# Attention values of two half-used row tiles, multiplied on two halves of the TensorE array

## The chip, the core and the metric

The kernel runs on one core of a Trainium2 chip. A core has five engines, each with its own instruction queue: TensorE (PE, matrix products; its weight loads are shown apart as PEld), VectorE (DVE), ScalarE (ACT), GpSimd (POOL) and SyncE (SP, which issues DMAs here). Matrix products write to PSUM, eight banks of 128 partitions × 512 fp32 values; DVE and ACT copy results from there to SBUF, the working memory. The metric is the device time in microseconds (us).

## The reference

A transformer block on x of shape (2, 512, 512), in fp32: attention, a layer norm of x plus its result, a gated feed-forward net of width 1376, and again a layer norm of the sum. The attention has 32 query heads of 128 values and 8 key/value heads, so four query heads share one key head:

```python
q = (x @ Wq.T).reshape(b, s, H, HD).transpose(0, 2, 1, 3)     # H = 32
k = (x @ Wk.T).reshape(b, s, HKV, HD).transpose(0, 2, 1, 3)   # HKV = 8
v = (x @ Wv.T).reshape(b, s, HKV, HD).transpose(0, 2, 1, 3)
q = _rmsnorm(q, q_norm_w)
k = _rmsnorm(k, k_norm_w)
scores = jnp.einsum('bkgqd,bksd->bkgqs', qg, k) / math.sqrt(HD)
bias = jnp.where(rel > 0, NEG_INF, slopes[:, :, None, None] * rel)
attn = jax.nn.softmax(scores + bias[None], axis=-1)
out = jnp.einsum('bkgqs,bksd->bkgqd', attn, v)
```

`rel` is key position minus query position: a query sees only keys up to its own place. What a product computes for later keys is nothing but zeros.

## The kernel before, in words

The sequence of 512 tokens is cut into four blocks of 128. A *unit* is (g, b, i): key head g (8), batch b (2), block i (4); there are 64 units. Two neighbouring units, i = 0 and 1 or i = 2 and 3, form a *pair* p, 32 in all; inside a pair r is 0 for the even block and 1 for the odd one.

For each pair, `project` computes queries, keys and values of both blocks, `heads` normalises and transposes them and copies the value rows into `v` (one 128 × 128 slab for each block, on ACT or POOL). `scores` and `attend` then run for each of the two units, and `project_out` multiplies the pair's attention result by the output weights and adds it to `y`. Projections use a seven-product scheme for 2 × 2 block matrices (`seven`, line 566), whose sums of operands (`so`, `to`, `tq`) and additions to results go through the helper at line 518 on DVE or POOL.

The 128 queries of a unit and their four heads make 512 rows of scores. They stand in four *row tiles* a = 0 to 3 of 128 rows: 32 neighbouring queries with all four heads. Row tile a of block i needs keys 0 to w = 128 i + 32 (a + 1), so on its own block of keys (the diagonal) tile 0 needs 32 keys, tile 1 needs 64, tile 2 needs 96 and tile 3 all 128. In `scores`, for each tile: a product into a bank `sc` (line 875), bias and maximum on DVE (line 884), exp and row sum on ACT (line 900); then a reciprocal `rden` of the four sums on DVE (line 915), and for each tile one multiplication by it on POOL (line 924), in place in `pr`. `pr` of block i has i + 1 slabs of 128 columns; what no tile writes was set to zero once at the start (line 479).

In `attend`, for each block of keys j up to i: four PE transposes, one for each tile, into a bank `pt` (line 943), and a copy of the whole bank to `prT` in SBUF (lines 641 on ACT or 643 on DVE). Then the products `pa` add up over j, each with 128 rows of values as weights and all 512 columns of `prT` moving (line 966); the result is copied, with a reordering of the columns, to `aT`, from which `project_out` reads. On the diagonal, too, all four tiles are transposed over 128 keys and multiplied with 128 rows of values.

PSUM: three banks `f` for projections, two `sc`, two `pt` (all transposes), one `po` (the attention results).

The order of the work is not that of the program text. Each piece is added to a list with the engines that may do it, an assumed cost, a priority, and the keys that it reads and writes; `emit` plays these through and hands out the piece that could start first, picks the engine, and takes buffers from rings as earlier holders are done. So a change in one piece can move others, on every engine, also in the feed-forward stage. DMAs go through SP's queue; the diff touches none.

Of the kernel before, what the change touches and what calls it, by code (L numbers as in the profile page):

```python
# [13 lines left out]
ALU = mybir.AluOpType  # L14
# [3 lines left out]
P = 128  # L18
B, S, DM = 2, 512, 512
H, HKV, HD = 32, 8, 128  # L20
G = H // HKV
# [9 lines left out]
NQ = P // Q  # L31
W3 = 3 * HD
WO = DM // 2
NTH = S // 2
RMS_EPS = 1e-6
LN_EPS = 1e-5
NEG_INF = -1e30
# [9 lines left out]
def pe(n):  # L47
    return max(0.14, n / 600)


TR = 0.107
# [14 lines left out]
def pool_ts(n):  # L66
    return 0.3 + 0.00095 * n
# [164 lines left out]
def post_ln_block(  # L232
# [18 lines left out]
    nc = tc.nc  # L251
# [4 lines left out]
    W = Work()  # L256
# [13 lines left out]
    def ring(stage, name, bufs, shape, dtype=F32, gate=None):  # L270
        r = Ring(name, bufs, shape, dtype, gate)
        rings.setdefault(stage, []).append(r)
        return r
# [6 lines left out]
    r_pt = ring("psum", "pt", 2, [P, S])  # L280
    r_po = ring("psum", "po", 1, [P, S])
# [33 lines left out]
    r_aT = ring("att", "aT", 2, [P, 2, G, P])  # L315
    r_so = ring("att", "so", 1, [P, 4, 2, P])
    r_rel = ring("att", "rel", 1, [P, S])
    r_pr = [ring("att", f"pr{i}", 1, [P, NQ, (i + 1) * P]) for i in range(NTB)]

    for stage, side in (("all", "left"), ("qkv", "left"), ("att", "right")):  # L320
# [8 lines left out]
    ident, nhalf, rel = fixed(r_id, "ident"), fixed(r_nh, "nhalf"), fixed(r_rel, "rel")  # L329
# [145 lines left out]
    for i in range(NTB):  # L475
        W.add(
            {"DVE": 0.1 + 0.00085 * NQ * (i + 1) * P},
            -8.0 + i,
            lambda e, i=i: nc.vector.memset(pr_of[i].tile, 0.0),
            (),  # L480
            [(pr_of[i], a) for a in range(NQ)],
        )

    bias = {}
# [148 lines left out]

    c_of, qTs, kTs, vs, prTs, aTs = {}, {}, {}, {}, {}, {}

    def copy_op(n, prio, dst, src, reads, writes, who=("ACT", "DVE")):
        def fn(e):
# [108 lines left out]
    def heads(p, prio):  # L748

        g, b, i = pairs[p]  # L750
        cb = c_of[p]
        c = lambda r: cb[:, r].rearrange("p n w -> p (n w)")
        if i == 0:
            kTs[g, b] = Buf(r_kT, f"kT_{g}_{b}")
            vs[g, b] = Buf(r_v, f"v_{g}_{b}")
        kT, v = kTs[g, b], vs[g, b]
        sq = Buf(r_sq, f"sq_{p}")
        ms, inv = Buf(r_ms, f"ms_{p}"), Buf(r_inv, f"inv_{p}")
        nh = 2 * (G + 1)
        for r in range(2):  # L760
            W.add(
                {"ACT": act(5 * HD) + 0.05},
                prio,
                lambda e, r=r: nc.scalar.activation(  # L764
                    sq[:, r].rearrange("p h d -> p (h d)"), c(r)[:, : 5 * HD], AF.Square
                ),
                [(cb, (r, 0)), (cb, (r, 1))],
                [(sq, r)],
            )
        W.add(  # L770
            {"DVE": 1.5},
            prio,
            lambda e: nc.vector.tensor_reduce(ms.tile, sq.tile, AX.X, ALU.add),
            [(sq, 0), (sq, 1)],
            [A(ms)],
        )
        W.add(
            {"DVE": 0.2},
            prio,
            lambda e: nc.vector.tensor_scalar(  # L780
                ms.tile, ms.tile, 1.0 / HD, RMS_EPS, ALU.mult, ALU.add
            ),
            [A(ms)],
            [A(ms)],
        )
        rsqrt(
            lambda: inv.tile.rearrange("p r h -> p (r h)"),
            lambda: ms.tile.rearrange("p r h -> p (r h)"),
            nh,
            prio,  # L790
            A(inv),
            A(ms),
        )
        for r in range(2):
            tensor(
                5 * HD,
                prio,
                lambda r=r: sq[:, r],
                lambda r=r: c(r)[:, : 5 * HD].rearrange("p (h d) -> p h d", h=G + 1),
                lambda r=r: inv[:, r].unsqueeze(2).to_broadcast([P, G + 1, HD]),  # L800
                ALU.mult,
                [(cb, (r, 0)), (cb, (r, 1)), A(inv)],
                [(sq, r)],
            )
            copy_op(
                HD,
                prio + 0.2,
                lambda r=r: v[:, i + r, :],
                lambda r=r: c(r)[:, 5 * HD :],
                [(cb, (r, 1))],  # L810
                [(v, i + r)],
                ("ACT", "POOL"),
            )
        for r in range(2):
            key = f"{g}_{b}_{i + r}"
            pt = Buf(r_pt, f"ptq_{key}")
            qT = Buf(r_qT, f"qT_{key}")
            qTs[g, b, i + r] = qT

            def transposes(e, r=r, pt=pt):  # L820
                for h, k in enumerate((0, 1, 3, 4)):
                    nc.tensor.transpose(pt[:, ts(h, P)], sq[:, r, k, :], ident.tile)  # L822

            W.add({"PE": 4 * TR}, prio + 0.4, transposes, [(sq, r), A(ident)], [A(pt)])

            def evict(e, pt=pt, qT=qT):
                src = pt.tile.rearrange("p (h a r) -> p a h r", h=G, a=NQ)
                if e == "ACT":
                    nc.scalar.activation(qT.tile, src, AF.Copy, scale=qw.tile)
                else:  # L830
                    nc.vector.tensor_scalar_mul(qT.tile, src, qw.tile)

            W.add(
                {"ACT": act(S, True), "DVE": dve(S) + 0.05},
                prio + 0.4,
                evict,
                [A(pt), A(qw)],
                [A(qT)],
            )
        ptk = Buf(r_pt, f"ptk_{p}")  # L840

        def transposes_k(e):
            for r in range(2):
                nc.tensor.transpose(ptk[:, ts(r, P)], sq[:, r, 2, :], ident.tile)

        W.add({"PE": 2 * TR}, prio + 0.4, transposes_k, [(sq, 0), (sq, 1), A(ident)], [A(ptk)])
        W.add(
            {"DVE": 0.48},
            prio + 0.4,
            lambda e: nc.vector.tensor_scalar_mul(  # L850
                kT[:, i * P : (i + 2) * P], ptk[:, : 2 * P], kw.tile
            ),
            [A(ptk), A(kw)],
            [(kT, i), (kT, i + 1)],
        )
# [3 lines left out]
    def scores(u, prio):  # L859
# [9 lines left out]
        for a in range(NQ):  # L869
# [46 lines left out]
            [(den, a) for a in range(NQ)],  # L916
            [A(rden)],
        )
        for a in range(NQ):
            w = i * P + (a + 1) * Q  # L920
            W.add(
                {"POOL": pool_ts(w)},
                prio,
                lambda e, a=a, w=w: nc.gpsimd.tensor_scalar(  # L924
                    pr[:, a, :w], pr[:, a, :w], rden[:, a : a + 1], 1.0, ALU.mult, ALU.mult
                ),
                [(pr, a), A(rden)],
                [(pr, a)],
            )

    def attend(u, prio):

        g, b, i = u
        key = f"{g}_{b}_{i}"
        pr, v = pr_of[i], vs[g, b]
        p, r = divmod(units.index(u), 2)
        for j in range(i + 1):
            pt, prT = Buf(r_pt, f"pt_{key}_{j}"), Buf(r_prT, f"prT_{key}_{j}")
            prTs[u, j] = prT

            def transposes(e, j=j, pt=pt):
                for a in range(NQ):
                    nc.tensor.transpose(pt[:, ts(a, P)], pr[:, a, ts(j, P)], ident.tile)  # L943

            W.add(
                {"PE": NQ * TR},
                prio,
                transposes,
                [(pr, a) for a in range(NQ)] + [A(ident)],
                [A(pt)],  # L950
            )
            copy_op(
                S,
                prio,
                lambda prT=prT: prT.tile,
                lambda pt=pt: pt.tile,
                [A(pt)],
                [A(prT)],
            )
        po = Buf(r_po, f"pa_{key}")  # L960
        for j in range(i + 1):
            prT = prTs[u, j]
            W.add(
                {"PE": pe(S)},
                prio + 0.4,
                lambda e, j=j, prT=prT: nc.tensor.matmul(  # L966
                    po.tile, lhsT=v[:, j, :], rhs=prT.tile, start=(j == 0), stop=(j == i)
                ),
                [A(prT), (v, j)] + ([A(po)] if j else []),
                [A(po)],  # L970
            )
        if r == 0:
            aTs[p] = Buf(r_aT, f"aT_{p}")
        aT = aTs[p]
        copy_op(
            S,
            prio + 0.4,
            lambda: aT[:, r].rearrange("p h (a r) -> p a h r", a=NQ),
            lambda: po.tile.rearrange("p (a h r) -> p a h r", a=NQ, h=G),
            [A(po)],  # L980
            [(aT, r)],
        )

# [24 lines left out]
    def project_out(p, prio):  # L1010
# [6 lines left out]
            lambda j: so[:, j],  # L1017
            lambda r, k: aT[:, r, 2 * k : 2 * k + 2, :],
            lambda j: (so, j),
            lambda r, k: [(aT, r)],  # L1020
        )

        def a_ap(f, ch):
            return aT[:, f[0], 2 * f[1] + ch, :] if isinstance(f, tuple) else so[:, f, ch, :]

        def a_keys(f):
            return [(aT, f[0])] if isinstance(f, tuple) else [(so, f)]

        def b_ap(f, ch):
            if isinstance(f, tuple):  # L1030
# [475 lines left out]
```

## Time and profile before

| What | Value |
|---|---|
| median of 3 runs | 1091.03 us (1090.96 to 1091.54) |
| the profiled execution's own time | 1091.2 us |
| its span | 1089.1 us |
| mean granted TensorE clock | 0.997 |
| transposes `pt` (line 943) | 640 |
| products `pa` (line 966), records | 320, all 128 × 512 |
| evictions `prT` | 107 on ACT, 587 ns each; 53 on DVE, 690 ns each |
| evictions `aT` | 38 on ACT, 586 ns each; 26 on DVE, 691 ns each |
| normalising on POOL (line 924) | 256, 627 ns each on average |

The span is the time from the first to the last instruction in the profile; the execution's own time is 2.1 us longer. A row of the groups reads: line, engine, operation, out<-in with shapes, count, then busy time and the mean length of one in ns, then how long the engine had been idle just before, and what ended that. Busy times of PE are modelled at their ends, so that the distance between two starts tells what an instruction costs there. In a table by stretches, the columns are the stretch, its length, and for PE, PEld, DVE, ACT and POOL the busy time and the number of instructions, then the granted clock, the DMA share and GB/s.

### The profile page before, as it was taken

How to read it: one execution, taken by the hardware profiler on the slowest of the kernel's cores; microseconds unless marked ns; L12 is line 12 of the kernel's file. 1: busy time of each engine (PE TensorE's matmuls, PEld its weight loads, DVE VectorE, ACT ScalarE, POOL GpSimd, SP SyncE). 2: the span in 40 equal slices, each digit the busy share in tenths (PEclk: the TensorE clock that was granted, in tenths of full speed). 3: DMA queues.
4: the chain of work that ended last, by engine and by line, in shares of the span. 5: the costliest groups of instructions: out<-in, count | busy, mean ns of one | idle time of the engine just before them, and what ended most of it. 6: DMA issues, size and time to landing. Idle time of an engine off the chain costs nothing.

```text
span 1089.1 us, 13052 instructions
## 1 busy us (share of the span) xinstructions
PE 1070.1 (98%) x4548; PEld 762.2 (70%) x4548; DVE 670.2 (62%) x1563; ACT 411.4 (38%) x1017; POOL 481.3 (44%) x600
## 2 busy tenths in 40 slices
PE   8999999999999999999999999999999999999997
PEld 5667676767676767676766666666666778887886
DVE  7756565656564656465656565657585666677554
ACT  2543334434434343444333434344444434433100
POOL 9444444344534453444344435454573443245130
PEclk9999999999999999999999999999999999999999
DMA  8210011001100120011001100100101013220011
GB/s 280 79 46 14 1 39 59 1 1 40 59 0 1 39 59 1 1 39 59 1 1 40 58 1 1 39 1 1 39 1 29 12 39 97 73 85 20 1 39 39
DMA packets 44144, 38.92 MB, mean 36 GB/s; under 512 B 3664, under 2 KB 36432, under 8 KB 44080
## 3 DMA queue, kind: packets, MB, share of 16 engines
q1 hardware_dynamic: 42352, 37.05, 11.0%
q10 hardware_dynamic: 1728, 1.05, 0.4%
q8 instruction: 36, 0.59, 0.2%
q14 instruction: 28, 0.23, 0.1%
HBM read 35.99 MB, written 2.10 MB: 35 GB/s over the span
## 4 chain that ended last, share of the span: by engine, by line
PE 86%; DVE 5%; POOL 5%; DMA 2%; ACT 1%; issue 1%; SPq 0%; POOLq 0%; DVEq 0%; ACTq 0%
PE pa_q L566 13%; PE pa L966 10%; PE sc L875 10%; PE pa_o L566 9%; PE pa_h L566 6%; PE pt L943 6%; PE pb_q L566 6%; PE pb_o L566 5%; PE pc_q L566 4%; PE pa_d L566 3%; PE pb_h L566 3%; PE ptq L822 2%; DVE tq L518 2%; PE pc_o L566 2%; POOL inv L504 2%; POOL pr L924 2%
## 5 line engine op out<-in xcount | busy, mean ns | idle before, releaser
L924 POOL TENSOR_SCALAR pr<-pr,rden 128x32 f32<-128x32 f32 (+15 forms) x256 | 155.8, 627 | 148.6 <-DVE rden L915 148.0
L900 ACT ACTIVATE pr<-pr,nmax 128x32 f32<-128x32 f32 (+15 forms) x256 | 131.9, 516 | 95.4 <-DVE nmax L884 95.2
L966 PE MATMUL pa<-prT,v 128*128 128x512 f32 x320 | 164.2, 595 | 0.0
L875 PE MATMUL sc<-kT,qT 128*128 128x160 f32 (+15 forms) x512 | 148.9, 402 | 0.0
L884 DVE CUSTOM_DVE_ANT_0 pr<-sc,bias 128x32 f32<-128x32 f32 (+15 forms) x256 | 108.9, 436 | 28.0 <-PE sc L875 25.3
L875 PEld LDWEIGHTS sc<-kT,qT 128*128 128x128 f32 x512 | 90.2, 190 | 47.8 <-issue 29.6
L641 ACT COPY c<-pa_q 128x384 f32<-128x384 f32 x101 | 48.3, 478 | 135.3 <-PE pa_q L566 130.4
L943 PEld LDWEIGHTS pt<-ident,pr 128*128 128x128 f32 x640 | 76.4, 141 | 26.7 <-issue 9.7
L943 PE MATMUL pt<-ident,pr 128*128 128x128 f32 x640 | 91.5, 275 | 0.9 <-POOL pr L924 0.3
L566 PE MATMUL pa_q<-tq,sx 128*128 128x384 f32 x248 | 90.4, 487 | 1.4 <-POOL pr L924 1.4
L641 ACT COPY prT<-pt 128x512 f32<-128x512 f32 x107 | 60.5, 587 | 79.1 <-PE pt L943 78.9
L504 POOL TENSOR_TENSOR inv<-ms,nhalf 128x10 f32<-128x10 f32 x32 | 62.9, 1965 | 53.4 <-DVE ms L780 53.2
L518 DVE TENSOR_TENSOR y<-y,pa_o 128x256 f32<-128x256 f32 x128 | 53.6, 419 | 50.7 <-PE pa_o L566 49.9
L643 DVE COPY prT<-pt 128x512 f32<-128x512 f32 x53 | 36.2, 690 | 61.8 <-PE pt L943 61.7
L764 ACT ACTIVATE sq<-c 128x640 f32<-128x640 f32 x64 | 47.2, 737 | 69.1 <-DVE c L518 67.3
L518 DVE TENSOR_TENSOR c<-pb_q,c 128x384 f32<-128x384 f32 x62 | 34.3, 554 | 61.9 <-PE pb_q L566 58.1
L966 PEld LDWEIGHTS pa<-prT,v 128*128 128x128 f32 x320 | 56.6, 190 | 22.0 <-issue 4.9
L643 POOL COPY v<-c 128x128 f32<-128x128 f32 x50 | 16.0, 321 | 124.1 <-DVE c L518 124.1
L566 PE MATMUL pa_o<-to,so 128*128 128x256 f32 x256 | 65.8, 380 | 0.3 <-POOL pr L924 0.3
L566 PEld LDWEIGHTS pa_q<-tq,sx 128*128 128x128 f32 x248 | 45.9, 192 | 27.5 <-POOL pr L924 2.6
L566 PEld LDWEIGHTS pa_o<-to,so 128*128 128x128 f32 x256 | 47.0, 190 | 20.2 <-issue 9.9
L641 ACT COPY gu<-pa_h 128x256 f32<-128x256 f32 (+1 forms) x88 | 32.1, 370 | 71.5 <-PE pa_h L566 54.8
(152 smaller groups left out, 2048.3 us busy)
## 6 DMA issues: line engine op xcount, KB each, us to landing
w<-in_wqt_dram SPq DMA_DIRECT2D x32, 256.0 KB, 4.2
wo<-in_wot_dram SPq DMA_DIRECT2D x8, 1024.0 KB, 5.5
wi<-in_gwt_dram SPq DMA_DIRECT2D x14, 256.0 KB, 2.8
wi<-in_uwt_dram SPq DMA_DIRECT2D x14, 256.0 KB, 3.2
wdi<-in_dwt_dram SPq DMA_DIRECT2D x10, 256.0 KB, 3.3
y<-in_x_dram SPq DMA_DIRECT2D x1, 2048.0 KB, 12.9
out_dram<-o SPq DMA_DIRECT2D x8, 256.0 KB, 2.0
w<-in_wkt_dram SPq DMA_DIRECT2D x7, 256.0 KB, 4.9
```

Source lines behind the costliest of these rows:

```text
L504: lambda e: nc.gpsimd.tensor_tensor(dst(), src(), nhalf[:, :n], ALU.pow),
L518: lambda e: vec[e].tensor_tensor(dst(), a(), b(), alu),
L566: nc.tensor.matmul(bank[:rows, :width], lhsT=a(fa, c), rhs=b(fb, c), start=(fresh and c == 0), stop=(c == depth - 1), skip_group_check=True,)
L641: nc.scalar.copy(dst(), src())
L643: vec[e].tensor_copy(dst(), src())
L764: lambda e, r=r: nc.scalar.activation(sq[:, r].rearrange("p h d -> p (h d)"), c(r)[:, : 5 * HD], AF.Square),
L875: lambda e, a=a, w=w, sc=sc: nc.tensor.matmul(sc[:, :w], lhsT=qT[:, a, :, :], rhs=kT[:, :w], start=True, stop=True),
L884: lambda e, a=a, w=w, sc=sc: nc.vector.tensor_tensor_reduce(out=pr[:, a, :w], in0=sc[:, :w], in1=bg[:, S - w :], scale=-1.0, scalar=MAX_IN ...
L900: lambda e, a=a, w=w: nc.scalar.activation(pr[:, a, :w], pr[:, a, :w], AF.Exp, bias=nmax[:, a : a + 1], scale=-1.0, accum_out=den[:, a : a ...
L924: lambda e, a=a, w=w: nc.gpsimd.tensor_scalar(pr[:, a, :w], pr[:, a, :w], rden[:, a : a + 1], 1.0, ALU.mult, ALU.mult),
L943: nc.tensor.transpose(pt[:, ts(a, P)], pr[:, a, ts(j, P)], ident.tile)
L966: lambda e, j=j, prT=prT: nc.tensor.matmul(po.tile, lhsT=v[:, j, :], rhs=prT.tile, start=(j == 0), stop=(j == i)),
```

## The change

Row tiles 0 and 1 need at most the first 64 keys of their own block. After the change these two tiles of the even block and of the odd block of a pair share one diagonal slab: that of the odd block, whose columns 64 to 127 are unused by its tiles 0 and 1. POOL's multiplication for tiles 0 and 1 of the even block writes the 64 diagonal columns there (into `pr` of the odd block) and, for i = 2, a second multiplication does the 256 earlier columns in place. The even block's diagonal then has two transposes in place of four; the odd block's four, in the order 2, 3, 0, 1, of which the last two carry both blocks: after transposing, rows 0 to 63 hold the odd block's keys and rows 64 to 127 the even block's.

The diagonal products `pa` take only tiles 2 and 3 (256 columns). Tiles 0 and 1 get two more products of 64 rows × 256 columns: rows 0 to 63 of the array with the odd block's values into a bank `px` (of the ring `pt`), and rows 64 to 127 with the even block's values into `pz` (of the ring `po`). For the second, the first 64 value rows of the even block are copied to partitions 64 to 127 (`v2`, on ACT or POOL). Both results are added to `aT` on DVE, but for the even block with i = 0, which has no earlier keys: there it is a copy.

```diff
+    r_vs = ring("att", "vs", 2, [P, HD])
...
+        v2 = Buf(r_vs, f"vs_{p}")
+        v2s[p] = v2
+        copy_op(
+            HD,
+            prio + 0.2,
+            lambda: v2[P // 2 :, :],
+            lambda: c(0)[: P // 2, 5 * HD :],
+            [(cb, (0, 1))],
+            [A(v2)],
+            ("ACT", "POOL"),
+        )
...
         for a in range(NQ):
             w = i * P + (a + 1) * Q
-            W.add(
-                {"POOL": pool_ts(w)},
-                prio,
-                lambda e, a=a, w=w: nc.gpsimd.tensor_scalar(
-                    pr[:, a, :w], pr[:, a, :w], rden[:, a : a + 1], 1.0, ALU.mult, ALU.mult
-                ),
-                [(pr, a), A(rden)],
-                [(pr, a)],
-            )
+            pieces = [(0, w, pr, 0, [(pr, a)])]
+            if i % 2 == 0 and a < 2:
+                pieces = [(i * P, H2, pr_of[i + 1], (i + 1) * P + H2, [(pr_of[i + 1], ("x", a))])]
+                if i > 0:
+                    pieces.append((0, i * P, pr, 0, [(pr, a)]))
+            for c0, n, to, c1, keys in pieces:
+                W.add(
+                    {"POOL": pool_ts(n)},
+                    prio,
+                    lambda e, a=a, c0=c0, n=n, to=to, c1=c1: nc.gpsimd.tensor_scalar(
+                        to[:, a, c1 : c1 + n],
+                        pr[:, a, c0 : c0 + n],
+                        rden[:, a : a + 1],
+                        1.0,
+                        ALU.mult,
+                        ALU.mult,
+                    ),
+                    [(pr, a), A(rden)],
+                    keys,
+                )
...
+            tiles = (2, 3) if j == i and r == 0 else (2, 3, 0, 1) if j == i else (0, 1, 2, 3)
...
+            def transposes(e, j=j, pt=pt, tiles=tiles):
+                for k, a in enumerate(tiles):
+                    nc.tensor.transpose(pt[:, ts(k, P)], pr[:, a, ts(j, P)], ident.tile)
...
+            n = S // 2 if j == i else S
             W.add(
-                {"PE": pe(S)},
+                {"PE": pe(n)},
                 prio + 0.4,
-                lambda e, j=j, prT=prT: nc.tensor.matmul(
-                    po.tile, lhsT=v[:, j, :], rhs=prT.tile, start=(j == 0), stop=(j == i)
+                lambda e, j=j, prT=prT, n=n: nc.tensor.matmul(
+                    po[:, S - n :],
+                    lhsT=v[:, j, :],
+                    rhs=prT[:, :n],
+                    start=(j == 0),
+                    stop=(j == i),
+                    skip_group_check=True,
                 ),
...
+        prT, v2 = prTs[u, i], v2s[p]
+        banks = (Buf(r_pt, f"px_{key}"), Buf(r_po, f"pz_{key}"))
+
+        def halves(e):
+            for k, (bank, val) in enumerate(zip(banks, (v[:, i, :], v2.tile))):
+                nc.tensor.matmul(
+                    bank[:, : S // 2],
+                    lhsT=val[k * H2 : (k + 1) * H2],
+                    rhs=prT[k * H2 : (k + 1) * H2, S // 2 :],
+                    start=True,
+                    stop=True,
+                    tile_position=(k * H2, 0),
+                )
+
+        W.add(
+            {"PE": 0.7},
+            prio + 0.4,
+            halves,
+            [A(prT), (v, i), A(v2)],
+            [A(bank) for bank in banks],
+        )
+        for k, bank in ((1, banks[0]), (0, banks[1])):
+            key_k = [(aT, (k, 0))]
+            if i - 1 + k == 0:
+                copy_op(
...
+            else:
+                tensor(
+                    S // 2,
+                    prio + 0.4,
+                    lambda k=k: cells(k, 0, 2),
+                    lambda k=k: cells(k, 0, 2),
+                    lambda bank=bank: rows(bank, 0, 2),
+                    ALU.add,
...
```

More of the change, by code (lines that the diff above doesn't have):

```diff
@@ L34 @@
 NTH = S // 2
+H2 = P // 2
 RMS_EPS = 1e-6
@@ L480, in post_ln_block @@
             (),
-            [(pr_of[i], a) for a in range(NQ)],
+            [(pr_of[i], a) for a in range(NQ)] + [(pr_of[i], ("x", a)) for a in range(2)],
         )
@@ L632, in sums_o @@
         )
-    c_of, qTs, kTs, vs, prTs, aTs = {}, {}, {}, {}, {}, {}
+    c_of, qTs, kTs, vs, v2s, prTs, aTs = {}, {}, {}, {}, {}, {}, {}
     def copy_op(n, prio, dst, src, reads, writes, who=("ACT", "DVE")):
@@ L939, in attend @@
             prTs[u, j] = prT
[L941 to L946, printed above, removed]
-                prio,
[L948 to L956, printed above, removed]
+            tiles = (2, 3) if j == i and r == 0 else (2, 3, 0, 1) if j == i else (0, 1, 2, 3)
+            reads = [(pr, a) for a in tiles]
+            if j == i and r:
+                reads += [(pr, ("x", a)) for a in range(2)]
+            def transposes(e, j=j, pt=pt, tiles=tiles):
+                for k, a in enumerate(tiles):
+                    nc.tensor.transpose(pt[:, ts(k, P)], pr[:, a, ts(j, P)], ident.tile)
+            n = len(tiles)
+            W.add({"PE": n * TR}, prio, transposes, reads + [A(ident)], [A(pt)])
+            copy_op(
+                n * P,
+                prio,
+                lambda prT=prT, n=n: prT[:, : n * P],
+                lambda pt=pt, n=n: pt[:, : n * P],
                 [A(pt)],
@@ L974, in attend @@
         aT = aTs[p]
+        a0 = 0 if i else 2
+        cells = lambda r, lo, hi: aT[:, r].rearrange("p h (a r) -> p a h r", a=NQ)[:, lo:hi]
+        rows = lambda t, lo, hi: t.tile.rearrange("p (a h r) -> p a h r", a=NQ, h=G)[:, lo:hi]
         copy_op(
-            S,
+            (NQ - a0) * P,
             prio + 0.4,
-            lambda: aT[:, r].rearrange("p h (a r) -> p a h r", a=NQ),
-            lambda: po.tile.rearrange("p (a h r) -> p a h r", a=NQ, h=G),
+            lambda: cells(r, a0, NQ),
+            lambda: rows(po, a0, NQ),
             [A(po)],
-            [(aT, r)],
+            [(aT, (r, h)) for h in range(a0 // 2, 2)],
         )
+        if r == 0:
+            return
+        prT, v2 = prTs[u, i], v2s[p]
[20 more added lines that the diff above has]
+            if i - 1 + k == 0:
+                copy_op(
+                    S // 2,
+                    prio + 0.4,
+                    lambda k=k: cells(k, 0, 2),
+                    lambda bank=bank: rows(bank, 0, 2),
+                    [A(bank)],
+                    key_k,
+                )
+            else:
+                tensor(
+                    S // 2,
+                    prio + 0.4,
+                    lambda k=k: cells(k, 0, 2),
+                    lambda k=k: cells(k, 0, 2),
+                    lambda bank=bank: rows(bank, 0, 2),
+                    ALU.add,
+                    [A(bank)] + key_k,
+                    key_k,
+                    ("DVE",),
+                )
     def accumulate(t, prio):
@@ L1019, in project_out @@
             lambda j: (so, j),
-            lambda r, k: [(aT, r)],
+            lambda r, k: [(aT, (r, 0)), (aT, (r, 1))],
         )
@@ L1026, in a_keys @@
         def a_keys(f):
-            return [(aT, f[0])] if isinstance(f, tuple) else [(so, f)]
+            return [(aT, (f[0], 0)), (aT, (f[0], 1))] if isinstance(f, tuple) else [(so, f)]
         def b_ap(f, ch):
```

## The prediction

> **What bounds the kernel now.** I read the totals first, then the chain that ended last, then the groups of the two steps concerned, then the timeline of TensorE for the real price of one instruction. The page's totals and chain:
>
> ```profile
> span 1089.1 us, 13052 instructions
> PE 1070.1 (98%) x4548; PEld 762.2 (70%) x4548; DVE 670.2 (62%) x1563; ACT 411.4 (38%) x1017; POOL 481.3 (44%) x600
> PE 86%; DVE 5%; POOL 5%; DMA 2%; ACT 1%; issue 1%; SPq 0%; POOLq 0%; DVEq 0%; ACTq 0%
> ```
>
> PE is busy for 98% of the span and carries 86% of the chain. The busy times of two stretches of the attention stage say how tight it is there (the second column is the length, the third PE busy):
>
> ```profile
> 100.00:300.00 200.00, 199.19 (x840) 135.98 (x839) 123.05 (x303) 81.45 (x209) 91.86 (x115) 1.00 0.09 27
> 500.00:700.00 200.00, 199.70 (x835) 135.93 (x834) 124.32 (x303) 80.98 (x208) 94.19 (x118) 1.00 0.09 27
> ```
>
> About 1 us of 400 is idle, at full clock. So a microsecond off PE in this stage is a microsecond off the end, and the others have slack (DVE about 62%). The groups that the change touches:
>
> ```profile
> L966 PE MATMUL pa<-prT,v 128*128 128x512 f32 x320 | 164.2, 595 | 0.0
> L943 PE MATMUL pt<-ident,pr 128*128 128x128 f32 x640 | 91.5, 275 | 0.9 <-POOL pr L924 0.3
> ```
>
> 160 products leave 320 matmul records, and as many weight loads: an fp32 product is two loads and two matmuls. Mean durations here overlap, since the modelled end of one lies beyond the start of the next; the price is the distance between starts, from the timeline of PE (start, length, what):
>
> ```profile
> 299.70 1.02 PE L966 MATMUL pa<-prT,v 128*128 128x512 f32 x2
> 300.56 0.60 PE L822 MATMUL ptq<-ident,sq 128*128 128x128 f32 x4
> 301.00 1.03 PE L566 MATMUL pa_o<-to,so 128*128 128x256 f32 x4
> 301.86 0.97 PE L875 MATMUL sc<-kT,qT 128*128 128x224 f32 x4
> ...
> 307.84 1.04 PE L943 MATMUL pt<-ident,pr 128*128 128x128 f32 x8
> 308.72 1.46 PE L566 MATMUL pa_q<-tq,xT 128*128 128x384 f32 x4
> ```
>
> A 512-column product costs 300.56 − 299.70 = 0.86 us, a 256-column record 0.86 / 4 = 0.215 (0.43 a product), a transpose 0.88 / 8 = 0.11. A record's modelled length minus its step (0.595 − 0.43) is a tail of 0.16. Where products are very short, loads set the pace:
>
> ```profile
> 343.55 0.58 PE L875 MATMUL sc<-kT,qT 128*128 128x64 f32 x4
> 343.97 1.05 PE L966 MATMUL pa<-prT,v 128*128 128x512 f32 x2
> ```
>
> Four records of 64 and 96 columns take 0.42: 0.105 a load.
>
> [...]
>
> **The change, part by part.** There are 32 pairs of token blocks.
>
> Removed from PE: the even block's diagonal no longer transposes tiles 0 and 1: 2 × 32 = 64 transposes × 0.11 = 7.0 us. The diagonal product of each of the 64 blocks shrinks from 512 to 256 columns: 64 × 0.43 = 27.5 us. Sum 34.5 us, 1.08 a pair.
>
> Added to PE: per pair two products of 64 rows × 256 columns, on rows 0-63 and 64-127, in two PSUM banks. As full products they would be 0.86 a pair. In program order they are load, matmul, load, matmul on the lower rows, then the same on the upper rows. With a strict order, the lower half's second matmul waits for its first, and the upper half's first can run only beside the lower half's second: three steps, 3 × 0.215 = 0.645, not two (0.43). Four loads × 0.105 = 0.42 fit beneath. Then two changes of mode a pair. The trace has none, so bounds: nothing, up to a whole tail and an exposed load each time, 2 × (0.16 + 0.19) = 0.70. A gain below nothing is excluded, as no work disappears with a switch. I take 0.16 for both together (each exposes half a tail, the loads go ahead as they do elsewhere). So 0.645 + 0.16 = 0.81 a pair, 25.9 us. The bounds of the pair are 0.43 and 0.86 + 0.70 = 1.56; it breaks even at 1.08.
>
> POOL (normalising, line 924): gone are 16 each of widths 32, 64, 288 and 320: 11.3 + 12.0 + 8.1 + 8.5 = 39.9 us. New are 64 of width 64, between 0.48 (the 256-wide row) and 0.75 (the 64-wide row), 31 to 48, and 32 of width 256 × 0.48 = 15; and 22 of the 32 copies of the value rows (10 are on ACT) at 0.32 (the v copies) = 7. POOL grows by 13 to 30 us from 481, in 1089: hidden behind PE. DVE gets 48 additions × 0.42 (the y additions of the same shape) = 20 us; prT and aT copies move between DVE and ACT for another few: about 690 of 1080. Hidden too; if the cover were gone, the additions alone would cost their 20 us.
>
> Waits. The two half products wait for the evicted transposes, the value copy, and both banks[...]. Placed in the built order with the step prices above, at least 1.29 us of PE work stands between the transposes and the half products (at least 1.19 before any product in the old order), against an eviction of 0.59 (ACT) or 0.69 (DVE). The single bank for attention outputs is now used by 96 products instead of 64: the work between its last writer and the half product that needs it is 0.35 once, 1.03 once, else 1.5 and more (least before: 2.17). So perhaps 0.5 us once or twice. What is late next would be the output projection, which has 4 to 6 us of other products to hide behind.
>
> The feed-forward stage is reordered by the planner. It holds one real hole:
>
> ```profile
> 982.87 2.02 PE L566 MATMUL pa_h<-tx,sw 128*96 128x256 f32 x4 [2.54 <-ACT gu L641]
> ```
>
> with the clock at 0.90 and 0.81 in the two 6 us stretches around it, 2.5 + 0.6 + 1.1 = 4.2 us. The late one is hT on DVE behind a 1.75 us weight sum; in the new order hT stands ahead of that sum. This could give up to 4.2, or the hole opens elsewhere. I count nothing and carry ±3 in the range.
>
> Sum: −34.5 + 25.9 = −8.6 on the profiled 1091.2 (span 1089.1 and 2.1 around it); the median 1091.03 is 0.2 lower: 1082.4 us.
>
> **The rivals.** *Drained switches:* if each of the 64 changes of mode costs over (1.08 − 0.645) / 2 = 0.22 us, the kernel gets slower. With the full 0.35: 0.645 + 0.70 = 1.35, +8.6 us, 1099.6. [...] Against: loads are hidden everywhere in this trace. *Not side by side:* if the halves run one behind the other (0.86) and the switches cost the same 0.16, the pair takes 1.02: −1.9 us, 1089, the change not doing what it says. *Full overlap:* if hardware interleaves the four matmuls, 0.43 and cheap switches: up to −20.8, 1070[...]. *PSUM:* with the attention bank shared by three products and one of two transpose banks held until an addition on DVE is done, PE could stall 0.3 us a pair, +10 us relative to the forecast, 1092; the distances above speak against.
>
> **How the numbers follow.** Three steps and moderate switches (0.65 to 0.95 a pair, 1077 to 1087): 0.50. Full overlap (1070 to 1076): 0.10. Not side by side: 0.17, which straddles the old time. Drained switches: 0.18. PSUM waits: 0.05. A difference under 0.2%, 2.2 us, can't be told from none. Faster: 0.50 + 0.10 + 0.06 = 0.66; within: 0.09 + 0.02 = 0.11; slower: 0.02 + 0.18 + 0.03 = 0.23. The range leaves out the far ends of full overlap and of drained switches: 1072 to 1099. The likeliest case's own range is 1077 to 1087.
>
> **What would show it.** The new products' first starts 0.215 apart, except the third beside the second; from the first half product's start to the next full-array matmul after the pair about 0.8; transposes 576; PE idle in the attention stage still near 0.3%; DVE near 690. I am wrong if the distance from the matmul before a pair to the first half, or from its last to the next, exceeds the normal step by over 0.2, if starts of the third and second are a full 0.215 apart, or if PE waits on the attention bank in many pairs.

## The result and the profile after

The changed kernel takes 1079.62 us (median of 4 runs, 1078.98 to 1081.15) against 1091.28 for the kernel before: ratio 0.9889, 95% interval 0.9876 to 0.9902, 11.7 us or 1.1% faster. The forecast was 1082.4 in a range of 1072 to 1099. Its total was nearly right; the reasoning under the price of the half products was not.

The profiled execution took 1081.15 us, the slowest of the four, with a span of 1079.4. Totals and chain of the page, as before:

```profile
span 1079.4 us, 13367 instructions
PE 1059.0 (98%) x4612; PEld 763.0 (71%) x4612; DVE 687.2 (64%) x1611; ACT 408.3 (38%) x1024; POOL 514.8 (48%) x673
PE 92%; DVE 4%; DMA 2%; POOL 1%; issue 1%; ACT 0%; SPq 0%; POOLq 0%; DVEq 0%; ACTq 0%
```

PE is still the bound: 98% busy, and a larger part of the chain (92%) than before. DVE came to 687 us (690 forecast) and POOL to 515 (494 to 511 forecast), both behind PE's cover. Two stretches of the attention stage, in the table by stretches:

```profile
100.00:300.00 200.00, 199.92 (x865) 137.81 (x864) 124.97 (x312) 84.56 (x216) 99.56 (x134) 1.00 0.09 27
500.00:700.00 200.00, 199.65 (x865) 138.61 (x864) 127.37 (x317) 82.28 (x214) 102.84 (x139) 1.00 0.09 27
```

PE idles for 0.4 us of 400. The two groups, and the transposes' number, as the change wants them (page):

```profile
L997 PE MATMUL pa<-prT,v 128*128 128x512 f32 (+1 forms) x320 | 136.3, 507 | 0.0
L978 PE MATMUL pt<-ident,pr 128*128 128x128 f32 x576 | 79.4, 273 | 0.3 <-DVE prT L645 0.3
```

`pa` lost 164.2 − 136.3 = 27.9 us and `pt` 12.1, 7 of it by number and the rest, as far as the trace tells, by waits between transposes, of which more below. What `pa` lost, the half products take again: 27.4 us, as the account will show. The new products, in the timeline of PE (start, length, what), one pair out of 32:

```profile
151.41 0.49 PE L568 MATMUL pb_q<-tq,sx 128*128 128x384 f32 x1
151.83 0.48 PE L1029 MATMUL px<-prT,v 64*128 64x256 f32 x1
151.84 0.48 PE L1029 MATMUL pz<-prT,vs 64*128 64x256 f32 x1
152.15 0.38 PE L1029 MATMUL px<-prT,v 64*128 64x256 f32 x1
152.16 0.38 PE L1029 MATMUL pz<-prT,vs 64*128 64x256 f32 x1
152.46 0.56 PE L889 MATMUL sc<-kT,qT 128*128 128x352 f32 x1
```

`px` on the lower rows and `pz` on the upper start 0.01 apart, both times, and so in 31 of the 32 pairs. The program's order is px, px, pz, pz; yet pz's first record runs beside px's first. So the halves overlap wholly: two steps, not three. But the distances around them are long. The record before has 384 columns, a step of 0.32 (the median behind such records), so that the next would start at 151.73: the pair starts 0.10 later. From the first record of `px` to its second it takes 0.32, where full-array records of 256 columns take 0.215. The second's 256 columns last, by that step, until 152.36; from there to the next product it is 0.10 again, and that product's first record takes 0.107 more than its columns, as `px`'s first did (the median of the 32 pairs). The weight loads of the same stretch, in the timeline of PEld, say what the 0.10 and the 0.107 are:

```profile
151.83 0.18 PEld L1029 LDWEIGHTS px<-prT,v 64*128 64x128 f32 x1 [0.55 <-issue]
151.84 0.18 PEld L1029 LDWEIGHTS pz<-prT,vs 64*128 64x128 f32 x1
151.94 0.19 PEld L1029 LDWEIGHTS px<-prT,v 64*128 64x128 f32 x1
151.94 0.19 PEld L1029 LDWEIGHTS pz<-prT,vs 64*128 64x128 f32 x1
152.46 0.30 PEld L889 LDWEIGHTS sc<-kT,qT 128*128 128x128 f32 x2 [0.33 <-issue]
```

PEld had been idle for 0.55 before the first half's load and for 0.33 before the next full one, and each of the two loads starts together with its matmul's record. In the kernel before, loads ran ahead under the matmul in front: the first load of the product that starts at 301.00 in the prediction's timeline starts at 300.89 (timeline of PEld, before), and the 762.2 us of loads lie beneath 1070.1 us of matmuls in a span of 1089.1.

```profile
300.89 0.73 PEld L566 LDWEIGHTS pa_o<-to,so 128*128 128x128 f32 x4
```

So a change of mode, from the whole array to its halves or back, cost here an empty stretch of 0.10 and then a load that nothing covers: the first record behind it is longer by 0.107, and two loads lie 0.108 apart there (medians of the 32 pairs). That is 0.205 a change, 0.41 a pair; with the two steps, 2 × 0.213 + 0.41, about 0.835.

**The account.** From the trace I took the distance between starts of each matmul record and its successor. Part of it is what its columns take, by estimate 0.833 ns a column: in the trace of before the median distance is 0.109 us behind a record of 128 columns and 0.429 behind one of 512, 0.320 for 384 columns more. The rest is waiting and loading, with the 2 to 3 ns by which these medians exceed their columns; 7.75 us before the first record and after the last are the same in both. Before, columns made 1037.0 us and the rest 44.35. After, all but the half products make 1002.9, which is 34.1 less (34.5 forecast): 6.8 for the 64 transposes and 27.3 for the diagonal products. The pairs make 27.4 (31 × 0.835, and one of 1.57), with the loads after them counted in. The rest is 41.3, 3.0 less. −34.1 + 27.4 − 3.0 = −9.7, as the spans of 1089.1 and 1079.4 say. So the diagonal products taken out and the half products put in cancel, 27.3 against 27.4; what is left of the gain is 6.8 us of transposes and 3.0 us of waits. The profiled execution also spent 3.4 us at half clock at 28 us (granted clock 0.50 from 28.2 to 31.6), which the one of before did not, by estimate a loss of up to 1.7 us, half of it; the other three executions had spans 1.5 to 2.2 us shorter.

The rest of 41.3 hides a gain and a loss. In the kernel before, transposes waited for POOL tile by tile (27 waits of about 0.23, 6.2 us in all). In the timeline of PE of before, four transposes take 1.18 between the starts where 0.44 is the price:

```profile
188.98 1.34 PE L943 MATMUL pt<-ident,pr 128*128 128x128 f32 x4
190.16 0.49 PE L566 MATMUL pa_q<-tq,sx 128*128 128x384 f32 x1
```

After, 0.3 us of such waits are left. About 3 us came elsewhere, spread over the start and the feed-forward stage. The hole in that stage, of which I had counted nothing, stayed: 2.54 became 2.83 (timeline of PE, after), ended by DVE in place of ACT. In the trace after, `hT` stands again behind a weight sum of 1.75 us on DVE, where the prediction had it ahead.

```profile
973.01 1.36 PE L568 MATMUL pb_h<-x1T,sw 128*96 128x256 f32 x4 [2.83 <-DVE gu L520]
```

### The profile page after: what moved, and what is told of

It reads as the page before. It is cut to its first block, busy times and chain, and to the rows that moved or that the text cites. A ratio compares the mean times of both kernels' runs of the same rounds, so it can differ in the third digit from the quotient of the medians.

```text
span 1079.4 us, 13367 instructions
## 1 busy us (share of the span) xinstructions
PE 1059.0 (98%) x4612; PEld 763.0 (71%) x4612; DVE 687.2 (64%) x1611; ACT 408.3 (38%) x1024; POOL 514.8 (48%) x673
## 3 DMA queue, kind: packets, MB, share of 16 engines
q10 hardware_dynamic: 1728, 1.05, 0.4%
## 4 chain that ended last, share of the span: by engine, by line
PE 92%; DVE 4%; DMA 2%; POOL 1%; issue 1%; ACT 0%; SPq 0%; POOLq 0%; DVEq 0%; ACTq 0%
PE pa_q L568 14%; PE sc L889 12%; PE pa_o L568 10%; PE pa L997 10%; PE pb_q L568 7%; PE pt L978 6%; PE pa_h L568 5%; PE pb_o L568 5%; PE pc_q L568 4%; PE pa_d L568 3%; PE pb_h L568 3%; PE ptq L836 3%; PE pc_o L568 2%; PE px L1029 2%; PE pb_d L568 2%; PE pc_h L568 1%
## 5 line engine op out<-in xcount | busy, mean ns | idle before, releaser
L946 POOL TENSOR_SCALAR pr<-pr,rden 128x64 f32<-128x64 f32 (+12 forms) x288 | 155.3, 558 | 83.6 <-DVE rden L929 71.3
L889 PE MATMUL sc<-kT,qT 128*128 128x160 f32 (+15 forms) x512 | 154.2, 407 | 0.3
L997 PE MATMUL pa<-prT,v 128*128 128x512 f32 (+1 forms) x320 | 136.3, 507 | 0.0
L889 PEld LDWEIGHTS sc<-kT,qT 128*128 128x128 f32 x512 | 87.0, 190 | 42.1 <-issue 25.6
L978 PEld LDWEIGHTS pt<-ident,pr 128*128 128x128 f32 x576 | 68.8, 141 | 23.7 <-issue 10.8
L978 PE MATMUL pt<-ident,pr 128*128 128x128 f32 x576 | 79.4, 273 | 0.3 <-DVE prT L645 0.3
L643 ACT COPY prT<-pt 128x512 f32<-128x512 f32 (+1 forms) x79 | 43.5, 556 | 78.9 <-PE pt L978 78.5
L645 DVE COPY prT<-pt 128x512 f32<-128x512 f32 (+1 forms) x81 | 50.0, 621 | 33.2 <-PE pt L978 32.7
L643 ACT COPY aT<-pa 128x512 f32<-128x512 f32 (+1 forms) x48 | 26.4, 550 | 87.8 <-PE pa L997 87.8
```

The source lines that it names most:

```text
L643: nc.scalar.copy(dst(), src())
L645: vec[e].tensor_copy(dst(), src())
L889: lambda e, a=a, w=w, sc=sc: nc.tensor.matmul(sc[:, :w], lhsT=qT[:, a, :, :], rhs=kT[:, :w], start=True, stop=True),
L946: lambda e, a=a, c0=c0, n=n, to=to, c1=c1: nc.gpsimd.tensor_scalar(to[:, a, c1 : c1 + n], pr[:, a, c0 : c0 + n], rden[:, a : a + 1], 1.0, ...
L978: nc.tensor.transpose(pt[:, ts(k, P)], pr[:, a, ts(j, P)], ident.tile)
L997: lambda e, j=j, prT=prT, n=n: nc.tensor.matmul(po[:, S - n :], lhsT=v[:, j, :], rhs=prT[:, :n], start=(j == 0), stop=(j == i), skip_group ...
```

## The experiments

All are compared with the kernel before, in runs shared on the same chip. Differences from the changed kernel go across runs; the medians of the kernel before in these runs, 1090.9 to 1091.3, agree within 0.4 us.

**Both halves on the same rows.**

```diff
-            for k, (bank, val) in enumerate(zip(banks, (v[:, i, :], v2.tile))):
+            for bank in banks:
                 nc.tensor.matmul(
                     bank[:, : S // 2],
-                    lhsT=val[k * H2 : (k + 1) * H2],
-                    rhs=prT[k * H2 : (k + 1) * H2, S // 2 :],
+                    lhsT=v[:H2, i, :],
+                    rhs=prT[:H2, S // 2 :],
...
-                    tile_position=(k * H2, 0),
+                    tile_position=(0, 0),
```

> Both half products are put on the lower 64 rows of the array, with the same weights and moving rows, so that they can't run beside each other; the mode changes stay. (The even block's tiles 0 and 1 thus get the odd block's values.) Theory A, from the trace of the changed kernel: the halves run wholly side by side (two steps of 0.213), and the two mode changes cost 0.41 a pair; then serial halves add 2 x 0.213 = 0.427 a pair, 13.6 us for 32: about 1093.3 us, back at the time of the kernel before. Theory B, that of the prediction: three steps and 0.16 for the switches; then one step more, 0.213 a pair, 6.8 us: about 1086.5. Theory C: the records only look simultaneous and the products run one behind the other anyway: 1079.6, no change.

1091.41 us; ratio to before 0.9998 (0.9990 to 1.0007): theory A, within 2 us. The timeline of PE in this run, where the second half now stands behind the first:

```profile
152.43 0.70 PE L1029 MATMUL px<-prT,v 64*128 64x256 f32 x2
152.96 0.59 PE L1029 MATMUL pz<-prT,v 64*128 64x256 f32 x2
153.48 0.56 PE L889 MATMUL sc<-kT,qT 128*128 128x352 f32 x1
```

From `px` to the product after the pair it is 1.05, in the changed kernel 0.63. Overlap is worth 0.42 a pair; without it, and with the mode changes, the whole change gained nothing.

**No array split.** The same two products over all 128 rows.

```diff
-            for k, (bank, val) in enumerate(zip(banks, (v[:, i, :], v2.tile))):
+            for bank in banks:
...
-                    lhsT=val[k * H2 : (k + 1) * H2],
-                    rhs=prT[k * H2 : (k + 1) * H2, S // 2 :],
+                    lhsT=v[:, i, :],
+                    rhs=prT[:, S // 2 :],
...
-                    tile_position=(k * H2, 0),
```

> The two half products become two products of all 128 rows x 256 columns, without a tile position, so there is no mode change and no product beside another. (Tiles 0 and 1 get sums over both blocks' values, which is not what is wanted.) Theory A (two steps side by side, 0.41 for the switches, 0.835 in all): a pair costs 4 x 0.215 = 0.86, so +0.03 a pair, +0.8 us: about 1080.5, no measurable loss from giving up the array split. Theory B (0.645 + 0.16): +0.055 a pair, +1.8 us, 1081.4. Theory D, that the array split is where most of the 11.7 us gain comes from: the loss of at least half of it, over 1085.

1080.12 us; ratio 0.9903 (0.9883 to 0.9923), not to be told from the changed kernel's 0.9889. Theory D is out; A and B lie too close for this run to choose between them. Timeline of PE:

```profile
151.94 0.59 PE L1029 MATMUL px<-prT,v 128*128 128x256 f32 x2
152.37 0.59 PE L1029 MATMUL pz<-prT,v 128*128 128x256 f32 x2
152.81 0.46 PE L889 MATMUL sc<-kT,qT 128*128 128x352 f32 x1
```

The pair takes 0.87, at the normal steps, without a gap before or after. So what the overlap wins (0.43), the two changes of mode take back (0.41). The gain of the change comes from elsewhere, and not from the diagonal products either: in this run they and the two full products have together the columns that the products had before (4 × 256 in place of 2 × 512 a pair), and still it is 11 us faster. It differs from the kernel before on PE in the 64 transposes and in the order alone. (That a kernel with right sums could do as well with full products follows only if the values that it needs, padded with zero rows, cost nothing on the path; it wasn't tried.)

**The pair twice in a row.**

```diff
-            for k, (bank, val) in enumerate(zip(banks, (v[:, i, :], v2.tile))):
+            for k, (bank, val) in 2 * list(enumerate(zip(banks, (v[:, i, :], v2.tile)))):
```

> The pair of half products is issued twice in a row, the second time over the same results; the result is the same. This is the price of a pair without the mode changes. Theory A: two steps more, 0.427 a pair, 13.6 us: about 1093.3. Theory B: three steps more, 0.645, 20.6 us: about 1100. Theory C (all serial): 0.86, 27.5 us: about 1107.

1092.23 us, ratio 1.001 (1.000 to 1.002): theory A, with 12.6 us for 13.6. In the timeline of PE only the first step of a stay is long:

```profile
126.06 0.48 PE L1029 MATMUL px<-prT,v 64*128 64x256 f32 x1
126.07 0.48 PE L1029 MATMUL pz<-prT,vs 64*128 64x256 f32 x1
126.39 0.38 PE L1029 MATMUL px<-prT,v 64*128 64x256 f32 x1
126.39 0.38 PE L1029 MATMUL pz<-prT,vs 64*128 64x256 f32 x1
126.60 0.38 PE L1029 MATMUL px<-prT,v 64*128 64x256 f32 x1
126.61 0.38 PE L1029 MATMUL pz<-prT,vs 64*128 64x256 f32 x1
126.82 0.38 PE L1029 MATMUL px<-prT,v 64*128 64x256 f32 x1
126.82 0.38 PE L1029 MATMUL pz<-prT,vs 64*128 64x256 f32 x1
127.13 0.55 PE L889 MATMUL sc<-kT,qT 128*128 128x32 f32 x3
```

0.32, then 0.215 each: a second pair cost two steps, and the loads inside the stay were hidden.

In one place of this run `pz` found its bank still in use, by ACT's copy (timeline of PE):

```profile
831.20 0.70 PE L1029 MATMUL px<-prT,v 64*128 64x256 f32 x2
831.95 0.48 PE L1029 MATMUL pz<-prT,vs 64*128 64x256 f32 x1
831.95 0.48 PE L1029 MATMUL px<-prT,v 64*128 64x256 f32 x1
832.27 0.38 PE L1029 MATMUL pz<-prT,vs 64*128 64x256 f32 x1
```

The first pair's two records of `px` ran ahead, but the second pair's `px`, which stands behind `pz` in the program, started only with `pz`, at 831.95. The trace shows no wait of its own for it, and by the steps (0.32 and 0.215 after 831.20) its rows were free at 831.74. So, where both banks were free, `pz`'s first record ran ahead of `px`'s second; here `px` did not run ahead of a `pz` that waited for its bank.

**Four changes of mode.** A full-array product between the halves.

```diff
                     tile_position=(k * H2, 0),
                 )
+                if k == 0:
+                    nc.tensor.matmul(
+                        bank[:, S // 2 : S // 2 + P],
+                        lhsT=v[:, i, :],
+                        rhs=prT[:, S // 2 : S // 2 + P],
+                        start=True,
+                        stop=True,
+                        skip_group_check=True,
+                    )
```

> A full-array product of 128 columns is put between the two half products, into columns of the bank that nobody reads; so there are four mode changes in place of two, and the halves stand alone. Theory A: two steps of 0.213 more for the halves, 0.215 for the extra product, and a second pair of switches at 0.41: 0.427 + 0.215 + 0.41 = 1.05 a pair, 33.7 us: about 1113. Theory B: one step more, 0.215, and 0.16: 0.59 a pair, 18.9 us: about 1098.5.

1112.32 us, ratio 1.020 (1.018 to 1.022), 32.7 above the changed kernel: theory A. The extra product, 0.215 by its 2 × 128 columns, takes 0.41 from its start to the next, its own bare load and the empty stretch behind it included (timeline of PE):

```profile
128.43 0.70 PE L1029 MATMUL px<-prT,v 64*128 64x256 f32 x2
129.06 0.49 PE L1038 MATMUL px<-prT,v 128*128 128x128 f32 x2
129.47 0.70 PE L1029 MATMUL pz<-prT,vs 64*128 64x256 f32 x2
130.10 0.66 PE L889 MATMUL sc<-kT,qT 128*128 128x32 f32 x4
```

**The removed transposes put back**, doing nothing.

```diff
-                for k, a in enumerate(tiles):
+                for k, a in enumerate(tiles * 2 if len(tiles) == 2 else tiles):
```

> The even block's two removed diagonal transposes are put back as two that nobody reads (tiles 2 and 3 again, into unused columns of the bank). If PE is the bound at every one, 64 x 0.109 = 7.0 us comes back: about 1086.6. If they lay under waits for POOL or the eviction, less than half of it: under 1083.

1085.69 us, ratio 0.9949 (0.9934 to 0.9963): 6.1 us for 64 transposes, 0.095 each. Nearly the full price; they were on the path, and they are half of the 11.7 us.

**Two pairs in one stay.** If a stay costs 0.41 and a further pair 0.43, pairs should be issued together. In `attend`, after the second pair of a key head and batch only:

```diff
-        if r == 0:
+        if i != NTB - 1:
             return
-        prT, v2 = prTs[u, i], v2s[p]
+        made = []
+        for q in (p - 1, p):
+            w = units[2 * q + 1]
+            made.append((q, w[2], prTs[w, w[2]], v2s[q]))
...
         def halves(e):
-            for k, (bank, val) in enumerate(zip(banks, (v[:, i, :], v2.tile))):
+            for m, (q, iq, prT, v2) in enumerate(made):
+                for k, (bank, val) in enumerate(zip(banks, (v[:, iq, :], v2.tile))):
...
-                    bank[:, : S // 2],
+                        bank[:, m * S // 2 : (m + 1) * S // 2],
```

> The half products of the two pairs of one key head and batch are issued together, after the second pair: eight 64-row records in one stay of the array in its split mode, so 16 stays in place of 32; the two results of a row half share one PSUM bank. The odd blocks' diagonal transposes get their own two buffers, aT and the shifted value rows one more each, and to make room qT and prT lose one, kT and v one each; the first pair's output projection waits for the second pair. Theory A: two pairs cost 4 x 0.213 + 0.41 = 1.26 in place of 2 x 0.835 = 1.67, 0.41 x 16 = 6.6 us less than the changed kernel: about 1073. Rival: the later output projection and the fewer buffers make PE wait for as much or more: 1079 or above, with PE waits in the attention stage of several us.

1074.38 us, ratio 0.9849 (0.9833 to 0.9866): 5.2 us below the changed kernel, of 6.6 expected. The timeline of PE:

```profile
175.22 0.81 PE L569 MATMUL pa_q<-w,xT 128*128 128x384 f32 x2
175.96 0.48 PE L1034 MATMUL px<-prT,v 64*128 64x256 f32 x1
175.97 0.48 PE L1034 MATMUL pz<-prT,vs 64*128 64x256 f32 x1
176.28 0.38 PE L1034 MATMUL px<-prT,v 64*128 64x256 f32 x1
...
176.71 0.38 PE L1034 MATMUL px<-prT,v 64*128 64x256 f32 x1
176.72 0.38 PE L1034 MATMUL pz<-prT,vs 64*128 64x256 f32 x1
177.02 0.70 PE L890 MATMUL sc<-kT,qT 128*128 128x160 f32 x3
```

By the distances between starts, and with the load after it, a stay of two pairs takes 1.27 (median of the 16; 1.26 expected). The buffers held longer did not make PE wait for more than the split saved: the attention stage's rest beyond the pairs (40 to 868 us) is 18.1 us, in the changed kernel 19.5; the feed-forward stage's grew by 3 us, in this order of its work. Here the array split pays: by estimate, the eight records as full-array ones, at 0.215 each, would take 1.72; that was not run.

**Order alone.** The planner's assumed price of a POOL multiplication, `0.3 + 0.00095 * n`, raised to 0.5 in the kernel before:

> The kernel before, with one number of the planner changed: the assumed fixed cost of a multiplication on POOL (line 924) is 0.5 in place of 0.3, so that only the order of the work differs. In the trace of before, transposes of a key head's first block wait for the POOL's tiles one after another, 27 waits of some 0.23, 6.2 us in all; in the changed kernel 0.3 us of it are left. If these waits come from the order (transposes planned too early), most of them go here too, and the time falls by 2 to 5 us, to 1086 to 1089. If POOL itself is late, or the change's fewer transposes on the diagonal took them away, they stay: 1091.

1087.21 us, ratio 0.9969 (0.9956 to 0.9982), 3.9 us faster with the same instructions. The transposes' waits for POOL are gone from the trace (0.1 us left of 6.2). But its profiled execution, at 1090.8 the slowest of its kernel, is no shorter than that of before: PE's rest in the attention stage is 3.2 us less, but 3.0 more came at the start (with 3.4 us at half clock at 28 us, as in the changed kernel) and in the feed-forward stage. So the trace doesn't prove that these waits were the 3.9 us. It shows that they hang on the order, and not on POOL or on how many transposes there are. It also gives an idea of how much of the change's 11.7 us is order: against the kernel before in this order, 1087.21, the changed kernel is 7.6 us faster, not far above the 6.1 of its transposes. The same edit was then made in the two newer kernels (in the changed one to 0.4).

> The changed kernel, with the planner's assumed fixed cost of a POOL multiplication at 0.4 in place of 0.3: another order, the same instructions. If order alone moves this kernel by a few us either way, the time differs from 1079.6 by 1 to 4 us with no common sign to the other reorderings; if it is better in general, 1076 or so; if the 3 us that the change gained beyond its own TensorE work are a lucky order, some of them go back here: 1081 to 1083.

1079.76 us, ratio 0.9894 (0.9875 to 0.9913): no difference.

> The batched kernel, with the planner's assumed fixed cost of a POOL multiplication at 0.5 in place of 0.3: another order, the same instructions. If the gain of the higher assumption in the kernel before (3.9 us) came from transposes of before waiting for POOL tile by tile, nothing is left to gain here, as the batched kernel shows no such waits: 1074.4 within 2. If a higher assumption is a better plan in general, 3 to 4 us less: about 1071.

1070.71 us, ratio 0.9819 (0.9798 to 0.9840): 3.7 us below the batched kernel, and the fastest of all, 20 us below the kernel before. Hardly any tile-by-tile waits were there to take away (0.6 us in the batched kernel's trace), so the reason given for the kernel before is not the whole of it. Which waits it removed was not followed up; of a raised price, two kernels gained about 4 us and one nothing.

## Why the prediction was right, and where it was not

*What bounds the kernel:* right. PE stayed at 98%, and every edit of PE's work in the runs was found again in the time, for the most part: 11.8 and 12.6 of 13.6, 32.7 of 33.7, 6.1 of 7.0, and 5.2 of 6.6 taken off.

*Removed work:* right. 34.5 forecast; the account's 34.1 is the same columns at nearly the same price, so it is no second measurement. Measured alone were the 64 transposes, at 0.095 against the 0.11 taken.

*The pair of half products:* the sum was right, 0.81 against 0.835, by luck: two errors cancelled. The step "in program order ... three steps, 3 × 0.215" failed: the strict order was my assumption, which no trace had shown, and between row halves it did not hold. In this trace `pz`'s first record, third in the program, runs beside `px`'s first, 0.01 behind it. The full overlap, given the low weight of 0.10 on that assumption alone, is what happened within the pair (0.43). The step "I take 0.16 for both together (... the loads go ahead as they do elsewhere)" failed too: the two changes cost 0.41, because the load after each was not hidden (0.107), on top of an empty 0.10. What a change costs no trace had shown; 0.16 was an estimate from tails and loads. Of the bounds, 0 to 0.70, the truth was past the middle. Neither rival was right alone: a change cost 0.205 of the 0.35 of "drained switches", just under the 0.22 from which, with three steps, the kernel would have become slower. The signs set beforehand fitted badly: from the first half product to the product after the pair it was 0.63, not 0.8; the two gaps stayed 0.10 over the normal step, under the 0.2 that was to mean an error; and the third and second starts lie 0.31 apart, which was to mean serial halves, because the third came first.

*Waits:* right. One pair of 32 found the attention bank still in use; its halves came apart, `px` at 821.16 and `pz` at 821.91 in the timeline of PE, and took 1.57. Nothing stands between the bank's last writer, `pa`, and this pair, so it is presumably the place counted with 0.35 us of work between; 0.74 lost where "perhaps 0.5 us once or twice" was said.

```profile
820.64 0.60 PE L997 MATMUL pa<-prT,v 128*128 128x256 f32 x2
821.16 0.70 PE L1029 MATMUL px<-prT,v 64*128 64x256 f32 x2
821.91 0.70 PE L1029 MATMUL pz<-prT,vs 64*128 64x256 f32 x2
```

*Missed:* 3.0 us in the profiled execution lie outside the change's own PE work: 5.9 us fewer waits of transposes for POOL, which a change of order alone also removes, and 2.9 us more elsewhere. The forecast had nothing for it, with ±3 in the range. The difference of 11.7 in the medians is larger than the 9.7 of the two profiled spans, since the one after was the slowest of its four.

*POOL:* 515 us lies just above the 494 to 511 forecast, but not by the terms forecast. The multiplications took 155.3 us, before 155.8, so they did not grow, and the copies of value rows brought 6.4; the rest of the 33.5 us is mostly other work that the planner gave to POOL, the squares `sq` above all (18 of them for 27.2 us, before 9 for 12.4). Nothing came of it.

## What to carry to other kernels

In this kernel a stay in the split mode cost 0.41 us for going in and out, with one pair in it (0.835) as with two (1.27); with 256 fp32 columns in each half the overlap was worth 0.43 a pair, so that a lone pair gained nothing, and two pairs in one stay did: with 16 stays in place of 32 the kernel took 5.2 us less. Before crediting a change with what it is named for, run it with the named part taken out: here the run without the split was as fast, the products that were saved and those that were added cancelled, and the gain lay in the transposes no longer done and in another order of the work. A total that comes out nearly right is no proof of its terms.

## What the runs showed that was not expected

- Matmuls on different row halves overtook each other against the program's order: with both banks free, px and pz started 0.01 apart (31 of 32 pairs) although px's second record stands between them in the program. But in the one place of the doubled run where pz waited for its bank, the px behind it waited too, and started with it at 831.95.
- In pace, a weight load of 64 rows cost what one of 128 rows does: 0.108 from load to load in the pairs; in the kernel before, the 128-row loads of the short products at 343.55 lie 0.110 to 0.112 apart, where the prediction took 0.105 for both, with no load of 64 rows measured. Two loads for different row halves started 0.01 apart, so they shared that time.
- A change of mode exposed 0.10 of emptiness and one load of 0.107, on the way in and on the way out; four changes in place of two added as much again (0.41 a pair).
- A changed assumption of the planner, with the same instructions, moved two kernels by 3.7 and 3.9 us of some 1080, a third of what the whole change gained.
